# A planner's order of feed-forward work, products per head group, narrow reciprocals and a layer norm aggregated on GpSimd, in a two-layer graph network on one core

## The chip, the core and the metric

The kernel runs on one core of a Trainium2 chip. The metric is the device time of one execution in microseconds; three executions of the kernel before took 3080.15, 3081.23 and 3081.99 us, so the median is 3081.23 us. The core's engines are TensorE (PE in the profile; its weight loads are PEld), VectorE (DVE), ScalarE (ACT), GpSimd (POOL) and SyncE (SP), which here issues the DMAs. Each takes its instructions in the order of the program and waits for the others on semaphores.

## The reference

64 graphs of 256 nodes with 256 features go through two layers. All arithmetic is in float32.

```
# layer 0: two graph attentions, then a feed-forward
h = gat(x, adj, W1, a1);  h = gat(h, adj, W2, a2)
    # gat: Wh = h @ W; e = leaky_relu(Wh @ a[:F] + (Wh @ a[F:]).T); masked where adj <= 0;
    #      softmax over axis 1; then att @ Wh
h = layernorm(x + h) * g_ln1 + b_ln1
x = layernorm(h + relu(h @ w_ff1 + b_ff1) @ w_ff2 + b_ff2) * g_ln2 + b_ln2
# layer 1: attention of 8 heads with a value matrix for each relation r = 0..3
attn = softmax(q k^T / sqrt(32))
out = sum over r of (attn * (adj == r)) @ (x @ Wv[r] + bv[r])
x = layernorm(x + out @ Wo + bo) * g1 + beta1
x = layernorm(x + gelu(x @ W1 + b1) @ W2 + b2) * g2 + beta2
```

The feed-forward layers are 1024 wide. The adjacency has only the values 0 and 1, so of the four relations two remain.

## The kernel before

**Tiling and stages.** The graphs are taken in 32 pairs. A pair goes through four stages: `gat_layers`, `feed_forward` of layer 0 (ReLU), `attention`, and `feed_forward` of layer 1 (GELU). A pair is one Python generator, `whole_way`; each `yield` ends one step of TensorE work and names what the next step waits for: events, a stage to be alone in ("gat", "ff" and "attention": one pair at a time), and the number of PSUM banks needed of eight.

**What sets the order.** `run` is a planner that runs when the program is built. It keeps a clock for every engine, goes through four pairs at a time (`together`), and chooses the next instruction by estimated times. TensorE steps come from the generators; everything else is a piece handed over by `put(engine, us, emit, *events, rank=...)`, where `us` is the estimated cost. Of the pieces that are ready on an engine, the lowest rank goes first, and among equals the one ready earliest. Of TensorE's steps that have been ready for `SLACK` = 0.3 us, line by line:

```
g = going[min(sure, key=lambda n: (going[n][0] is besides, "ff" in (going[n][2] or ()) or alone.get("ff") is going[n][0], n))
          if sure else min(times)[1]]
```

So the pair that is in a feed-forward, in any part of it, comes after all other pairs. The order found is then fixed by `keep_order`: every engine executes it as it stands, whatever the actual times are.

**Feed-forward.** Its first product (FF1, line 689) is made in blocks with seven products in place of eight, class `Blocks`: p1 to p7, twice (`a` and `b`, two slabs each), in the order of line 710. p6 waits for the copy of p1's result (`copy`, line 695, on ACT), p7 for p6's copy, p4 for p7's copy; p5 and p3 wait for additions on DVE (line 393). Activations are at line 701. The second product (FF2, line 720) is for each graph b two halves j of eight matrix products, ordered in two parts of four; it waits for activations only in the first graph. Right after the products of a graph, its sum with the rows (`add_rows`, line 571) and its layer norm are handed to the planner. A float32 matrix product counts as two matmul instructions in the profile.

**Layer norm.** `layernorm` handles one graph, two tiles of 128 rows: on DVE `bn_stats` and `bn_aggr` for each tile (lines 581 and 582), on GpSimd four small operations on 128x2 values (lines 587 to 590; line 589 is the power -0.5), on ACT the normalisation (line 594). Then `transposed` turns the rows on DVE in 32x32 blocks (line 623, into the single buffer `yb`), stores them to DRAM and gathers them back by four DMAs on SP (line 628 and after); `scaled` (line 604) applies gain and bias on GpSimd. For a few pairs at the start and the end (`hurried`), the transposition is made on TensorE (line 655) instead.

**Attention.** q, k and v are made with `Blocks` too (lines 764 and 769). `scores(n)` handles a group of four heads of one graph, n = 0 to 3: 16 tiled matmuls of 32 rows (line 809) into four banks; ACT's Exp in two halves of two activations (line 818, tile `a`); on DVE the mask and the sums of halves (lines 822 and 826, tiles `m` and `h`). `products(n)` makes 80 tiled matmuls of 32 columns: line 840 for the values, line 843 for the sums with a matrix of ones, whose result stands in 32 equal rows for each head. Then DVE's reciprocal of 256 columns (line 852), the product (line 853), and on ACT a `check` of the sums' size (line 850), which reads both the sums and the reciprocals and frees the bank. The products are planned in twos: products(0) and products(1) in one step when all their masks are there, then scores(2) and scores(3), then products(2) and products(3).

At the end a flag is computed from the checks; for the present inputs it leaves the second, general program unused.

Of the kernel before, what the change touches and what calls it, by code (L numbers as in the profile page):

```python
# [27 lines left out]
HURRIED = 2  # L28
SLACK = 0.3
# [4 lines left out]
def two_layers(ctx: ExitStack, tc: tile.TileContext, t: dict, out: bass.AP, flag: bass.AP):  # L34
# [74 lines left out]

    w12 = const.tile([P, KC, D + 4], F32, name="w12")  # L110
# [31 lines left out]
    alone = {}  # L142
# [16 lines left out]
    def put(engine, us, emit, *events, rank=1, lag=0.2, kb=0, function=None, needs=None, frees=(), event=None):  # L159

        piece = {"engine": engine, "us": us, "emit": emit, "rank": rank, "lag": lag, "kb": kb, "function": function,
                 "needs": needs, "frees": frees, "event": event or Event(), "ready": 0.0, "missing": 0}
        for e in events:
            if e.time is None:
                piece["missing"] += 1
                e.then.append(piece)
            else:
                piece["ready"] = max(piece["ready"], e.time)  # L170
        if not piece["missing"]:
            waiting[engine].append(piece)
        return piece["event"]

# [39 lines left out]
    def run(besides, ways, together):  # L214
# [3 lines left out]
        going, ways = [[besides, *next(besides)]], iter(ways)  # L218
        together += 1
        while True:  # L220
# [23 lines left out]
            if engine == "tensor":  # L244
                sure = [n for at, n in times if at <= now - SLACK]
                g = going[min(sure, key=lambda n: (going[n][0] is besides, "ff" in (going[n][2] or ()) or alone.get("ff") is going[n][0], n))
# [11 lines left out]
            else:  # L258
                piece = waiting[engine].pop(min(able, key=lambda n: (waiting[engine][n]["rank"], waiting[engine][n]["ready"])))
# [77 lines left out]

    def block_sums(w, there):
# [34 lines left out]
    class Blocks:  # L373
# [5 lines left out]
        def __init__(self, second, first, begin, multiply, target, copy, corner, finished):  # L379
# [18 lines left out]
        def p1(self):  # L398
            yield *self.first, 1
            self.begin()  # L400
            self.u1 = self.copy(0, 0, self.product(1, "x", 0, True))

        def p2(self):
            yield [], None, 1
            there = self.product(2, "z", 1, True)
            self.c11 = self.add(0, 0, "z", self.u1, there)
            self.second.read_by_second(there)

        def p5(self):
            yield [self.c11, self.second.there[0]], None, 0  # L410
# [20 lines left out]
        def p3(self):  # L431
            yield [self.c22], None, 0
            self.add(0, 1, "z", self.u2, self.product(3, "z", 5), frees=["bank"])
# [56 lines left out]
    def gat_weights(y, at, at_home, ratio, there, to, b):  # L490
# [16 lines left out]
        def scale():  # L507
            for j in range(2):
                k = 2 * b + j
                nc.scalar.activation(y[:, k, :at], y[:, k, :at], AF.Copy, scale=of["rs"][:, j:j + 1])  # L510

        there = put("vector", 1.03, lambda: weigh(0), *there, rank=b / 2, needs="e")
        there = put("vector", 1.11, lambda: weigh(1), there, rank=b / 2, frees=["rows"] * b)
        return of, put("scalar", 0.8, scale, there, rank=0)
# [58 lines left out]
    def layernorm(r, b, *events):  # L573
        st = mv = rstd = less = None
        rows = [r[:, 2 * b + j, :] for j in range(2)]

        def statistics():
            nonlocal st, mv
            st, mv = small.tile([P, 2, 6], F32, name="st"), small.tile([P, 2, 2], F32, name="mv")
            for j in range(2):  # L580
                nc.vector.bn_stats(st[:, j, :], rows[j])  # L581
                nc.vector.bn_aggr(mv[:, j, :], st[:, j, :])  # L582

        def root():
            nonlocal rstd, less
            rstd, less = small.tile([P, 2], F32, name="rstd"), small.tile([P, 2], F32, name="less")
            nc.gpsimd.tensor_scalar(less, mv[:, :, 0], -1.0, None, ALU.mult)  # L587
            nc.gpsimd.tensor_scalar(rstd, mv[:, :, 1], EPS, None, ALU.add)
# [3 lines left out]
        def normalise():  # L592
            for j in range(2):
                nc.scalar.activation(rows[j], rows[j], AF.Identity, bias=less[:, j:j + 1], scale=rstd[:, j:j + 1])  # L594

        there = put("vector", 0.9, statistics, *events)
        there = put("gpsimd", 1.5, root, there, rank=0)
        return put("scalar", 0.8, normalise, there)
# [67 lines left out]
    def feed_forward(y, normal, w, func, relieved, pair, stage):  # L666

        w1, b1, w2 = w
# [3 lines left out]
        f, evacuated = [None] * NF, [[None] * NF for _ in range(2)]  # L672
# [5 lines left out]
        def slabs(t):  # L678

            rows, columns = [], (slice(0, N), slice(N, 2 * N))  # L680

            def begin():
                for c in range(2):
                    rows.append(work.tile([P, 2, 512], F32, name="ff", bufs=NF // 2))
                    for n in range(2):
                        f[t + n + c * half] = rows[c][:, n]
# [4 lines left out]
            def target(c, h):  # L691
                return rows[c][:, :, columns[h]]
# [4 lines left out]
            def activate(c, h, event, of=None):  # L697
                for n in range(2):
                    m, to = t + n + c * half, rows[c][:, n, columns[h]]
# [3 lines left out]
                        frees=["bank"] * (n and of is not None))  # L703

            first = ([normal[0], normal[1], relieved, second.there[0]], ["ff"]) if t == 0 else ([], None)
            blocks = Blocks(second, first, begin, multiply, target, copy, lambda of, event: activate(1, 0, event, of), activate)
# [5 lines left out]
        order, end = (0, 1, 4, 5, 2, 3, 6, 7), b.p3  # L712
        for b in range(2):
            for j in range(2):
                for part in (order[:half], order[half:]):
                    yield [evacuated[j][m] for m in part] if b == 0 else [], None, j == 0 and part[0] == 0
                    if j == 0 and part[0] == 0:
                        p2 = bank()
                    for m in part:
                        nc.tensor.matmul(p2[:, j * D:(j + 1) * D], lhsT=f[m][:, (2 * j + b) * P:(2 * j + b + 1) * P],  # L720
                                         rhs=w2[:, m, :], start=m == 0, stop=m == NF - 1)
                    there = took(0.43 * len(part))
                    if b == j == 0 and part[0] == 0:
                        yield from end()
                        frees_at(clock["tensor"], ["yT", "sums_yT"])
            normal[b] = layernorm(y, b, add_rows(y, p2, b, there, normal["scaled", b]))
            if onwards:
                transposed(y, normal[b], normal, b, pair, 1)
            else:
                normal[b] = scaled(y, ln[3], b, normal[b])  # L730
        done_with("ff")


    def attention(y, normal, pair, all_adj):
# [66 lines left out]
        def scores(n):  # L801
# [9 lines left out]
            there = took(1.08)  # L811
# [3 lines left out]
            def weight(q):  # L815
                a[n][q] = work.tile([P, 2, 512], F32, name="a", bufs=HQ)
                for k in range(2):
                    nc.scalar.activation(a[n][q][:, k], ps[2 * q + k], AF.Exp)  # L818
# [5 lines left out]
            def halves(q):  # L824
# [3 lines left out]
            there = [put("scalar", 0.96, lambda q=q: weight(q), there, rank=0, function="exp", needs="a", frees=["bank"] * 2)  # L828
                     for q in range(HQ // 2)]
# [3 lines left out]
        def products(n):  # L833
# [10 lines left out]
            there = took(2.2)  # L844
            frees_at(there.time, ["a", "m"] * (HQ // 2) + ["h"] * (HQ // 2 - 1))
            s, to = h[n][0][:, 0], qk[:, 0, c, b * N:(b + 1) * N]

            def check():
                for of, c in ((s, 0), (po[:, N:], 1)):
                    nc.scalar.activation(of, of, AF.Copy, accum_out=reach[:, pair, c, n:n + 1])  # L850

            there = put("vector", 1.68, lambda: nc.vector.reciprocal(s, po[:, N:]), there, rank=0)  # L852
            there = put("vector", 0.34, lambda: nc.vector.tensor_tensor(to, po[:, :N], s, ALU.mult), there, rank=0)
            put("scalar", 1.0, check, there, frees=["bank", "h"])
            return there
# [579 lines left out]
```

## Time and profile before

| Engine | busy, us | share of the span |
|---|---|---|
| TensorE matmuls | 3010.9 | 98% |
| TensorE weight loads | 2454.7 | 80% |
| VectorE | 2234.0 | 73% |
| ScalarE | 1835.1 | 60% |
| GpSimd | 1032.2 | 34% |

The profiled execution took 3077.64 us, and its span, from the first to the last instruction, is 3075.9 us. TensorE's granted clock was 0.994 of full speed over the span.

| Line, engine | what | count | busy, us | mean, ns |
|---|---|---|---|---|
| L720 PE | second feed-forward products, both layers | 4096 | 466.4 + 461.7 | 380 |
| L581 DVE | bn_stats | 512 | 208.4 | 407 |
| L582 DVE | bn_aggr | 512 | 93.2 | 182 |
| L587, L588 POOL | tensor-scalar on 128x2 | 256 each | 65.4, 60.1 | 255, 235 |
| L589 POOL | power on 128x2 | 256 | 189.1 | 739 |
| L590 POOL | product on 128x2 | 256 | 52.7 | 206 |
| L852 DVE | reciprocal of 256 columns | 128 | 224.1 | 1752 |
| L850 ACT | checks, two activations and two reads of sums | 128 | 53.0, 47.4, 24.6, 23.8 | 414, 370, 192, 186 |

A "busy" time of TensorE is the union of the matmuls' spans, which overlap; a mean is that of one matmul from its start to its modelled end. "A <- B: t, n, m" in a view of waits says that A's engine sat idle for t us in n places, m at the longest, until B released it. In the timeline a line gives the start, the duration, the engine, the line in the code and the number of merged instructions, and in brackets the idle time before it.

### The profile page before, as it was taken

To read this page: it belongs to the slowest core of one execution; us is meant where nothing else is said; L and a number is where in the kernel's file an instruction comes from. 1 tells how busy PE (TensorE), PEld (TensorE's weight loads), DVE (VectorE), ACT (ScalarE), POOL (GpSimd) and SP (SyncE) were. 2 spreads that over 40 slices of the span, in tenths; PEclk is the share of its full clock that TensorE was granted. 3 is DMA by queue.
4 is the path that set the end of the run, shared out by engine and by line. 5 is a ranking of instruction groups with operands and counts; after the bars stand their busy time and mean duration, and the time that the engine had idled before them with its cause. 6 is when DMAs were issued, how large, how long until landed. Compare 5 with 4: busy or idle time off the path is not lost.

```text
span 3075.9 us, 52423 instructions
## 1 busy us (share of the span) xinstructions
PE 3010.9 (98%) x19154; PEld 2454.7 (80%) x19154; DVE 2234.0 (73%) x4411; ACT 1835.1 (60%) x4186; POOL 1032.2 (34%) x1542
## 2 busy tenths in 40 slices
PE   7999999999999999999999999999999999999998
PEld 6877778877878788887888778878788778788876
DVE  5787766788776867768677676686776777767774
ACT  4556665656665566565756566565666565655654
POOL 1332244232423243232352322533325333233223
PEclk8999999999999999999999999999999999999999
DMA  6211132102321122211231122311213211121000
GB/s 181 73 51 36 56 124 79 46 28 75 109 66 50 61 76 80 73 49 56 76 99 60 42 70 69 97 66 50 66 54 96 82 53 57 62 93 58 32 1 22
DMA packets 211865, 205.76 MB, mean 67 GB/s; under 512 B 22928, under 2 KB 171280, under 8 KB 211600
## 3 DMA queue, kind: packets, MB, share of 16 engines
q1 hardware_dynamic: 211184, 202.06, 20.5%
q8 instruction: 154, 2.52, 0.3%
q14 instruction: 111, 0.91, 0.1%
q10 hardware_dynamic: 416, 0.26, 0.0%
HBM read 137.51 MB, written 64.73 MB: 66 GB/s over the span
## 4 chain that ended last, share of the span: by engine, by line
PE 79%; DVE 10%; ACT 3%; DMA 3%; POOL 2%; issue 2%; SPq 1%; DVEq 0%; POOLq 0%; ACTq 0%
PE ps L720 24%; PE ps L689 20%; PE ps L840 6%; PE ps L764 6%; PE ps L769 6%; PE ps L809 4%; PE ps L545 3%; PE ps L529 3%; PE ps L862 2%; PE ps L843 2%; DVE e L502 2%; DVE x L571 2%; DVE st L581 1%; PE ps L558 1%; DMA home<-yb 1%
## 5 line engine op out<-in xcount | busy, mean ns | idle before, releaser
L587 POOL TENSOR_SCALAR less<-mv 128x2 f32<-128x2 f32 x256 | 65.4, 255 | 1596.6 <-DVE mv L582 1561.4
L594 ACT ACTIVATE x<-x,less,rstd 128x256 f32<-128x256 f32 x512 | 279.3, 594 | 418.8 <-POOL less L590 414.9
L720 PE MATMUL ps<-w_L_gnn_w_ff,ff 128*128 128x256 f32 x2048 | 466.4, 380 | 0.0
L720 PE MATMUL ps<-w_L_gnn_W,ff 128*128 128x256 f32 x2048 | 461.7, 380 | 0.9 <-ACT ff L701 0.9
L720 PEld LDWEIGHTS ps<-w_L_gnn_W,ff 128*128 128x128 f32 x2048 | 386.9, 190 | 61.0 <-issue 5.4
L720 PEld LDWEIGHTS ps<-w_L_gnn_w_ff,ff 128*128 128x128 f32 x2048 | 387.9, 190 | 57.2 <-issue 4.3
L393 DVE TENSOR_TENSOR ff<-ps,ff 128x512 f32<-128x512 f32 x384 | 261.1, 683 | 163.6 <-PE ps L689 127.1
L822 DVE TENSOR_TENSOR m<-a,adj 128x1024 f32<-128x1024 f32 x256 | 325.4, 1271 | 20.6 <-ACT a L818 20.5
L689 PE MATMUL ps<-yT,w_L_gnn_W1p 128*128 128x256 f32 x1280 | 316.1, 384 | 10.9 <-ACT ff L695 7.4
L689 PE MATMUL ps<-yT,w_L_gnn_w_ff1p 128*128 128x256 f32 x1280 | 312.4, 384 | 12.3 <-ACT ff L695 12.3
L818 ACT ACTIVATE a<-ps 128x512 f32<-128x512 f32 x512 | 266.8, 603 | 68.0 <-PE ps L809 67.1
L689 PEld LDWEIGHTS ps<-yT,w_L_gnn_W1p 128*128 128x128 f32 x1280 | 238.3, 190 | 61.8 <-ACT ff L695 17.9
L689 PEld LDWEIGHTS ps<-yT,w_L_gnn_w_ff1p 128*128 128x128 f32 x1280 | 241.3, 191 | 56.6 <-ACT ff L695 16.7
L571 DVE TENSOR_TENSOR x<-ps,x 128x512 f32<-128x512 f32 x256 | 173.0, 680 | 152.4 <-PE ps L720 120.3
L695 ACT ACTIVATE ff<-ps 128x512 f32<-128x512 f32 x384 | 221.1, 589 | 92.0 <-PE ps L689 90.1
L604 POOL TENSOR_TENSOR x<-x,b_L_gnn_g_ln 128x512 f32<-128x512 f32 x128 | 168.7, 1318 | 274.5 <-DVE yb L623 138.3
L852 DVE RECIPROCAL h<-ps 128x256 f32<-128x256 f32 x128 | 224.1, 1752 | 49.1 <-PE ps L843 48.9
L581 DVE BATCH_NORM_STATS2 st<-x 128x6 f32<-128x256 f32 x512 | 208.4, 407 | 4.7 <-issue 0.4
L701 ACT ACTIVATE ff<-ff,c_L_gnn_b_ff 128x256 f32<-128x256 f32 x384 | 174.4, 509 | 49.4 <-DVE ff L393 48.8
L604 POOL TENSOR_TENSOR x<-x,b_L_gnn_g 128x512 f32<-128x512 f32 x128 | 166.1, 1298 | 94.4 <-ACT x L594 74.8
L589 POOL TENSOR_TENSOR rstd<-rstd,mhalf 128x2 f32<-128x2 f32 x256 | 189.1, 739 | 21.3
L701 ACT ACTIVATE ff<-ff,c_L_gnn_b 128x256 f32<-128x256 f32 x384 | 172.0, 502 | 31.6 <-DVE ff L393 31.0
(138 smaller groups left out, 5499.8 us busy)
## 6 DMA issues: line engine op xcount, KB each, us to landing
home<-yb SPq DMA_DIRECT2D x182, 256.0 KB, 2.0
yT<-home SPq DMA_DIRECT2D x728, 64.0 KB, 2.0
rows<-row SPq DMA_DIRECT2D x60, 512.0 KB, 3.8
input<-in_xT SPq DMA_DIRECT2D x32, 512.0 KB, 4.0
x<-in_x SPq DMA_DIRECT2D x32, 512.0 KB, 4.1
out<-x SPq DMA_DIRECT2D x32, 512.0 KB, 2.9
input<-in_adjT SPq DMA_DIRECT2D x30, 512.0 KB, 4.1
v<-in_adjT SPq DMA_DIRECT2D x2, 512.0 KB, 6.6
```

The lines of the kernel that those rows point to most:

```text
L393: nc.vector.tensor_tensor(self.target(c, h), self.bank[bank], self.target(c, h), ALU.add)
L571: return put("vector", 0.6, lambda: nc.vector.tensor_tensor(rows, p, rows, ALU.add), *events, frees=["bank"])
L581: nc.vector.bn_stats(st[:, j, :], rows[j])
L594: nc.scalar.activation(rows[j], rows[j], AF.Identity, bias=less[:, j:j + 1], scale=rstd[:, j:j + 1])
L604: nc.gpsimd.tensor_tensor(both, both, v.rearrange("p (k d) -> p k d", k=1).to_broadcast([P, 2, D]), op)
L689: nc.tensor.matmul(to, lhsT=w1[:, a, (t + slab) * P:(t + slab + 1) * P], rhs=b, **flags)
L695: return put("scalar", 0.5, lambda: nc.scalar.activation(target(c, h), blocks.bank["x"], AF.Copy), event, rank=-1)
L701: evacuated[h][m] = put("scalar", 0.4, lambda m=m, to=to, source=source: nc.scalar.activation(to, source, func, bias=b1[:, m:m + 1]), even ...
L720: nc.tensor.matmul(p2[:, j * D:(j + 1) * D], lhsT=f[m][:, (2 * j + b) * P:(2 * j + b + 1) * P], rhs=w2[:, m, :], start=m == 0, stop=m == N ...
L818: nc.scalar.activation(a[n][q][:, k], ps[2 * q + k], AF.Exp)
L822: nc.vector.tensor_tensor(m[n][q], a[n][q], adj, ALU.mult)
L852: there = put("vector", 1.68, lambda: nc.vector.reciprocal(s, po[:, N:]), there, rank=0)
```

## The change

- **Order of the feed-forward.** A pair that is in FF1 now comes before all other pairs, one that has reached FF2 (it stands in `filling`) after all others. FF1's tiles are laid out by block (c, h) and not by slab; FF2 is moved into `by_eight`, and both graphs' layer norms are handed over after both graphs' products.
- **Attention.** products(n) are steps of their own, each waiting only for its own masks; scores(2) follows products(0) and scores(3) products(1). scores(0) is planned after a_.p3 and b_.p4.
- **Reciprocals.** The sums are transposed in 32x32 blocks on DVE, one column of each block is copied (8 columns), inverted, and transposed back with a broadcast. The checks read the 8 columns, and the bank is freed by the product.
- **Layer norm.** bn_aggr is left out; nine small operations on GpSimd combine the two halves of bn_stats' result.
- **Pieces.** `put_each` hands over a piece in parts, each a piece of its own that keeps the first one's place: Exp, the scaling of the attention rows (`gat_weights`), statistics and normalisation. Some estimated costs differ.
- **Code that no stage uses.** `SEVEN` is empty, so `by_seven`, `last_weights` and `last_sums` aren't called, and no `Blocks` has a `seed`. The scratch of dynamic DMAs is set to 1024 bytes a partition.

```diff
-    def put(engine, us, emit, *events, rank=1, lag=0.2, kb=0, function=None, needs=None, frees=(), event=None):
+    def put(engine, us, emit, *events, rank=1, lag=0.2, kb=0, function=None, needs=None, frees=(), event=None, behind=None):
...
+        piece["first"] = behind.piece["first"] if behind else piece
+        piece["event"].piece = piece
...
+    def put_each(engine, us, emits, *events, rank=1, frees=(), needs=None, function=None):
+
+        before = None
+        for emit in emits[:-1]:
+            before = put(engine, us, emit, *events, rank=rank, lag=0.0, needs=needs, function=function, behind=before)
+            events, needs = [before], None
+        return put(engine, us, emits[-1], *events, rank=rank, frees=frees, function=function, behind=before)
+
...
+        def degree(g):
+            if g[0] in filling:
+                return 2
+            return 0 if "ff" in (g[2] or ()) or alone.get("ff") is g[0] else 1
...
-                g = going[min(sure, key=lambda n: (going[n][0] is besides, "ff" in (going[n][2] or ()) or alone.get("ff") is going[n][0], n))
+                g = going[min(sure, key=lambda n: (going[n][0] is besides, degree(going[n]), n))
...
-                piece = waiting[engine].pop(min(able, key=lambda n: (waiting[engine][n]["rank"], waiting[engine][n]["ready"])))
+                piece = waiting[engine].pop(min(able, key=lambda n: (waiting[engine][n]["rank"], waiting[engine][n]["first"]["ready"])))
...
-                nc.vector.bn_aggr(mv[:, j, :], st[:, j, :])
...
-            nc.gpsimd.tensor_scalar(less, mv[:, :, 0], -1.0, None, ALU.mult)
-            nc.gpsimd.tensor_scalar(rstd, mv[:, :, 1], EPS, None, ALU.add)
+            halves = [st[:, :, 3 * n + 1:3 * n + 3] for n in range(2)]
+            nc.gpsimd.tensor_tensor(apart, halves[0][:, :, 0], halves[1][:, :, 0], ALU.subtract)
+            nc.gpsimd.tensor_tensor(both, *halves, ALU.add)
+            nc.gpsimd.tensor_tensor(apart, apart, apart, ALU.mult)
+            nc.gpsimd.tensor_scalar(rstd, both[:, :, 1], 1.0 / D, EPS, ALU.mult, ALU.add)
+            nc.gpsimd.tensor_scalar(apart, apart, 0.25, None, ALU.mult)
+            nc.gpsimd.tensor_scalar(less, both[:, :, 0], -0.5, None, ALU.mult)
+            nc.gpsimd.tensor_tensor(rstd, rstd, apart, ALU.add)
             nc.gpsimd.tensor_tensor(rstd, rstd, mhalf[:, :2], ALU.pow)
             nc.gpsimd.tensor_tensor(less, less, rstd, ALU.mult)
...
-        there = put("vector", 0.9, statistics, *events)
-        there = put("gpsimd", 1.5, root, there, rank=0)
-        return put("scalar", 0.8, normalise, there)
+        there = put_each("vector", 0.35, [lambda j=j: statistics(j) for j in range(2)], *events)
+        there = put("gpsimd", 2.7, root, there, rank=0)
+        return put_each("scalar", 0.5, [lambda j=j: normalise(j) for j in range(2)], there)
...
+        yield from (by_seven if stage in SEVEN else by_eight)(y, normal, f, evacuated, w2, w2_there, b)
+        for g in range(2):
+            normal[g] = layernorm(y, g, *normal["added"][g])
+            if onwards:
+                transposed(y, normal[g], normal, g, pair, 1)
+            else:
+                normal[g] = scaled(y, ln[3], g, normal[g])
+        filling.clear()
+        done_with("ff")
+
+    def by_eight(y, normal, f, evacuated, w2, w2_there, last):
+
+        half, order, normal["added"] = NF // 2, (0, 1, 4, 5, 2, 3, 6, 7), []
+        filling.append(alone["ff"])
+        for g in range(2):
             for j in range(2):
                 for part in (order[:half], order[half:]):
...
+            normal["added"].append([add_rows(y, p2, g, there, normal["scaled", g])])
...
-            there = took(1.08)
+            there = took(1.13)
...
-            there = [put("scalar", 0.96, lambda q=q: weight(q), there, rank=0, function="exp", needs="a", frees=["bank"] * 2)
-                     for q in range(HQ // 2)]
+            there = [put_each("scalar", 0.48, [lambda q=q, k=k: weight(q, k) for k in range(2)], there, rank=0, function="exp",
+                              needs="a", frees=["bank"] * 2) for q in range(HQ // 2)]
...
-            there = took(2.2)
+            there = took(2.34)
...
+            def invert():
+                both.append(small.tile([P, 2, N // 32], F32, name="inverse", bufs=4))
+                nc.vector.transpose(s, po[:, N:])
+                nc.vector.tensor_copy(both[0][:, 1], blocks[:, :, 0])
+                nc.vector.reciprocal(both[0][:, 0], both[0][:, 1])
+                nc.vector.transpose(blocks, both[0][:, 0].rearrange("p (g i) -> p g i", i=1).to_broadcast([P, N // 32, 32]))
...
-            there = put("vector", 1.68, lambda: nc.vector.reciprocal(s, po[:, N:]), there, rank=0)
-            there = put("vector", 0.34, lambda: nc.vector.tensor_tensor(to, po[:, :N], s, ALU.mult), there, rank=0)
-            put("scalar", 1.0, check, there, frees=["bank", "h"])
-            return there
+            there = put("vector", 1.3, invert, there, rank=0)
+            put("scalar", 0.4, check, there, rank=3)
+            return put("vector", 0.34, lambda: nc.vector.tensor_tensor(to, po[:, :N], s, ALU.mult), there, rank=0, frees=["bank", "h"])
...
-        for step in (a_.p1, b_.p1, a_.p2, a_.p6, b_.p2, a_.p5, b_.p6, a_.p7, b_.p5, a_.p4, b_.p7, lambda: scores(0), a_.p3, b_.p4,  b_.p3, lambda: scores(1)):
+        for step in (a_.p1, b_.p1, a_.p2, a_.p6, b_.p2, a_.p5, b_.p6, a_.p7, b_.p5, a_.p4, b_.p7, a_.p3, b_.p4, lambda: scores(0), b_.p3, lambda: scores(1)):
...
-        for n in (0, 2):
-            yield [*masked[n], *masked[n + 1], ready["v", 0, n // 2], ready["v", 1, n // 2]], None, 2
-            divided += [products(n), products(n + 1)]
-            if n == 0:
-                for later in (2, 3):
-                    yield from scores(later)
+        for n in range(4):
+            yield [*masked[n], ready["v", 0, n // 2], ready["v", 1, n // 2]], None, 1
+            divided.append(products(n))
+            if n < 2:
+                yield from scores(n + 2)
```

## The prediction

> **What bounds the kernel now.** I read the page's first part, then PE's waits after the first 100 us, then the order of time around the places where PE stands or changes its kind of work, and last the chain of waits at the end.
>
> ```profile
> PE 3010.9 (98%) x19154; PEld 2454.7 (80%) x19154; DVE 2234.0 (73%) x4411; ACT 1835.1 (60%) x4186; POOL 1032.2 (34%) x1542
> ...
> PE ps L689 <- ACT ff L695: 23.5, 31, 1.7
> PE ps L545 <- ACT xw L510: 2.6, 1, 2.6
> ...
> PEld ps L689 <- ACT ff L695: 44.3, 55, 2.1
> ```
>
> TensorE is the bound; no other engine is near. So the change can gain only the time in which PE stands, and it loses whatever it adds to PE. From the trace's start times, a full-array matmul pass follows the last after 216 ns (four in 0.86 us). Counting all that stands over this between full-array passes gives 51 us after the first 100 us: 44 at L689 (the first feed-forward product), 7 elsewhere. The weight loads' 44.3 us are the same stall as PE's 23.5: a weight load held by a wait costs about 0.3 us on top of the wait. The first 100 us hold another 22 us of such stalls and the last PE instruction ends 12.6 us before the end of the span.
>
> One such stall, of 1.5 us, in order of time:
>
> ```profile
> 1316.57 1.08 ACT L594 ACTIVATE x<-x,less,rstd 128x256 f32<-128x256 f32 x2
> ...
> 1317.56 0.90 ACT L701 ACTIVATE ff<-ff,c_L_gnn_b_ff 128x256 f32<-128x256 f32 x2
> 1318.35 1.06 ACT L695 ACTIVATE ff<-ps 128x512 f32<-128x512 f32 x2
> 1318.50 1.28 POOL L604 TENSOR_TENSOR x<-x,b_L_gnn_g_ln 128x512 f32<-128x512 f32 x1
> 1318.99 0.73 PEld L689 LDWEIGHTS ps<-yT,w_L_gnn_w_ff1p 128*128 128x128 f32 x4 [1.75 <-ACT ff L695]
> 1318.99 1.13 PE L689 MATMUL ps<-yT,w_L_gnn_w_ff1p 128*128 128x256 f32 x4 [1.34 <-ACT ff L695]
> ```
>
> The copy that PE needs (L695) stands in ACT's queue behind two normalisations (L594), and the chain of waits leads from those through four layer norms in a row on GpSimd (L587 to L590, each 1.65 us from start to start). PE has nothing else planned there. In the steady part the same stalls come back every 374 us, that is with every four pairs of graphs (1317, 1691, 2066, 2441).
>
> Tiled products and full-array products in order of time on PE:
>
> ```profile
> 1011.07 1.07 PE L840 MATMUL ps<-a,v 128*32 128x256 f32 x16
> 1011.96 1.05 PE L840 MATMUL ps<-m,v 128*32 128x256 f32 x16
> 1012.82 0.61 PE L843 MATMUL ps<-h,ones 128*32 128x256 f32 x8
> 1013.25 1.05 PE L840 MATMUL ps<-a,v 128*32 128x256 f32 x16
> ...
> 1015.53 1.99 PE L862 MATMUL ps<-w_L_gnn_Wo,qk 128*128 128x256 f32 x8
> 1017.36 1.92 PE L529 MATMUL ps<-w,input 128*128 128x260 f32 x8
> ```
>
> The first group of heads takes 2.18 us to the start of the second, the second 2.28 to the start of L862, and L862's eight passes take 1.83 where 8 x 0.216 is 1.73. So leaving the tiled form costs 0.10 + 0.10, and entering it, by the trace's starts, 309 ns instead of 216, 0.09.
>
> The end, from the chain of waits:
>
> ```profile
> 3063.28 0.69 DVE x L571
> ...
> 3065.34 0.22 POOL less L587
> ...
> 3066.94 0.49 ACT x L594
> ...
> 3068.11 1.26 POOL x L604
> ```
>
> **What the Trainium skill says.** "TensorEngine Tiling (Array Packing)", Key Properties: a change of the tiling mode drains TensorE. The trace agrees: 0.09 us in, 0.20 out. "PSUM — Partial Sum Buffer", Engine vs sequencer instructions: the queues of ScalarE, VectorE and GpSimd are strict FIFO; the stall above, a copy behind a normalisation that waits for GpSimd, is that. "ScalarE: Activation LUTs", What ACT_TABLE_LOAD costs: 1283 ns for a load; the trace has 1283 too, 96 times. "VectorE: DVE Perf Modes", The TRN2 errata — SBUF-src ops pay a fixed extra latency per instruction: a fixed cost for each instruction, then a cost per element. The trace agrees: a transpose of 64 columns takes 240 ns and one of 512 takes 702.
>
> **The change part by part.** The sum is made against the profiled execution, 3077.64 us (span 3075.9, 1.7 around it); the median of the runs is 3081.23, 3.6 above. No matmul is removed or added. by_seven, last_weights, last_sums and the seed path are called only for stages in SEVEN, which is empty: nothing. The smaller scratch of the DMA setting: POOL issues no DMA in this trace, so I take nothing, between -1 and +1.
>
> *Order of the feed-forward.* Now every step of a feed-forward stands behind all other pairs' work, so it runs when nothing else is there, and the stalls of its dependent products (p6, p7, p4 wait for copies) lie bare. Afterwards p1 to p4 go first, with other pairs' steps left over to fill their waits, and the second products, 13.8 us without any wait (64 passes), come last and serve as a reserve. The 64 feed-forwards take 12 to 25 us for the first part today where its 56 passes need 12.1. At best all of the 51 us goes. Against that: at the end of a reserve the other pairs are all blocked, so the next first part may again find no filler. I take half, -26; bounds 0 and -45.
>
> *Products per head group.* L840/L843's 128 groups stand in 64 back-to-back pairs. If each pair is split by full-array work, one more exit and entry come in: 0.10 + 0.10 + 0.09, about 0.3 us, x 64 = +20. But scores(n + 2) may now follow products(n) directly if four banks are free, which saves the exit's second half and the entry, 0.2 us, up to twice a pair of graphs: 64 x 0.2 = 13 less (eight such neighbours exist already, so 11). Bounds +9 and +20, I take +13.
>
> *Layer norm on GpSimd.* bn_aggr goes from DVE (512 x 182 ns = 93 us). L587 to L590's four small operations (255 + 235 + 739 + 206 = 1.43 us) become nine: three of the tensor-scalar kind at about 0.24, five at 0.21, the power 0.74 = 2.5 us, and 0.07 us between neighbours. One layer norm thus holds GpSimd for 3.05 us instead of 1.65, its latency grows by 1.4 less 0.4 for the aggregations, +1.0. GpSimd's load is 1032 + 256 x 1.07 = 1306 us, 42%: no bound. In the middle other pairs' work on PE hides it; without that cover it is what blocks ACT's queue in the stall shown. At the start, pair 0's first norm lies bare: +1.
>
> *Norms after both halves.* Today the first half's norm is put out before the second half's products, afterwards after them. The transposes share one yb buffer and one SP queue (store, then four gathers a half), so a stage's hand-over lengthens by some 3 to 5 us; three other pairs hide that, and if not, the price is that of the slower rival. At the end nothing hides it. Today: last product, add, statistics, 1.6 on GpSimd, normalise, two scalings of 1.26. Afterwards the first norm's GpSimd part ends about 2.4 us after the last product, the second's runs 3.05 to about 5.4 after it, and four scalings of 1.34 follow (10.8) where today's last ends 7.5 after it: +3.
>
> *Reciprocals of 8 columns.* L852 (1752 ns) becomes two transposes of 256 columns (between the 240 and 702 ns rows: 0.44 each), a copy and a reciprocal of 8 columns (near L505's 166 ns): 1.25. DVE -0.5 x 128 = -64 us; DVE falls to about 2077. The checks (L850) shrink on ACT from 1.16 to 0.78 us: -49 us. Banks and h are free before the check. All beside PE: 0, and part of why half the stalls may go.
>
> *Pieces.* Exp, scalings, statistics and normalisations become two pieces each, so an urgent copy waits for one activation (0.6) and not for two. Against it, a Gelu may fall between two Exps: each such turn is two loads of 1.28 us on ACT, which has 40% to spare. 0, between -3 and +5.
>
> Sum: -26 + 13 + 1 + 3 = -9, about 3069 against 3077.64 and 3072 against the median.
>
> **The rivals.** *Slower: mode changes and the longer norm.* All 64 pairs of products are split (+20), the end costs +3, the start +1; and GpSimd's 3.05 us per norm, of which two now come in a row exactly when the next feed-forward's first products run, holds ACT's normalisations and the copies behind them. The planner books 2.7, so two in a row are 0.7 late. If each of the 64 feed-forwards pays that, less the 0.3 us of slack that it plans with, that is +26 and eats the order's -26: 3081 + 24 = 3105. Where half of them pay, 3092. It decides once the remaining stalls exceed 51 - 24 = 27 us. For it: GpSimd's chain already ends in the stall shown, and ACT waits 414.9 us for it. Against it: most norms have other work ahead.
>
> *A wash.* A third of the stalls goes (-17), which +13 + 4 eat: 3081. For it: the steady pattern loses only about 1.3 us for each pair of graphs, and PE is at 99% there.
>
> *Twice the gain.* Nearly all stalls go (-45) and scores follow products (+9 + 4): 3049. For it: the last feed-forward of all, which runs alone and without others' work on ACT, stalls for under 1 us.
>
> **How the numbers follow.** Faster at about half the stalls 0.43, nearly all 0.09, a wash 0.19, slower 0.29. The likeliest one's own range is 3062 to 3076. Ten per cent at each side are cut off: 3048 to 3100. About 0.2% (6 us) is what can be told from no change: faster 0.51, same 0.20, slower 0.29.
>
> **What would show it.** Right: PE's waits for L695's successor and the weight loads' 44.3 us halved; 64 or more separate clusters of tiled products; the last product to the end 15 to 16 us instead of 12.6; DVE near 2080 and GpSimd near 1300 us. Wrong: the weight loads' waits at the first products as large as now or larger, with ACT standing before its normalisations for GpSimd; new waits of PE at attention's products; or the products still in pairs.

## The result, and the profile after

The changed kernel takes 3064.08 us (median of four, 3063.49 to 3066.88) against 3081.61 us for the kernel before, run beside it: a ratio of 0.9952, 95% interval 0.994 to 0.9964. The prediction said 3072, between 3048 and 3100. The profiled execution went from 3077.64 to 3063.49 us, its span from 3075.9 to 3061.6, 14.3 us less; the prediction's sum was 9 less.

From the page of the changed kernel, the engines' busy time:

```profile
PE 3007.5 (98%) x19154; PEld 2451.5 (80%) x19154; DVE 2114.7 (69%) x4283; ACT 1771.4 (58%) x4182; POOL 1265.7 (41%) x2822
```

PE's waits after the first 100 us (total us, how many, the longest):

```profile
PE ps L731 <- ACT ff L737: 15.6, 12, 2.0
PE ps L731 <- DVE ff L424: 1.6, 4, 0.4
```

And those of the weight loads:

```profile
PEld ps L731 <- ACT ff L737: 25.6, 25, 2.4
```

L731 is what L689 was, L737 the copy that was L695. The weight loads' wait for the copies fell from 44.3 us in 55 places to 25.6 in 25. What held the copies changed too. From each such copy one can walk back along ACT's queue to the last instruction before which ACT stood idle. Before, 19.8 of the 44.3 us led to a normalisation (L594) that waited for GpSimd. Now 19.8 of the 25.6 lead to a scaling of attention rows (L551) that waited for VectorE, 3.7 to an activation that waited for VectorE, and 1.8 to a normalisation. Now the kinds of work on PE, from the timeline of the changed kernel:

```profile
533.27 1.07 PE L960 MATMUL ps<-a,v 128*32 128x256 f32 x16
534.15 1.05 PE L960 MATMUL ps<-m,v 128*32 128x256 f32 x16
535.02 0.61 PE L963 MATMUL ps<-h,ones 128*32 128x256 f32 x8
535.56 1.15 PE L929 MATMUL ps<-qk 32*128 32x256 f32 x16
536.64 1.07 PE L960 MATMUL ps<-a,v 128*32 128x256 f32 x16
...
540.01 3.72 PE L778 MATMUL ps<-w_L_gnn_w_ff,ff 128*128 128x256 f32 x16
543.57 2.75 PE L731 MATMUL ps<-yT,w_L_gnn_w_ff1p 128*128 128x256 f32 x12
```

A group's products are followed at once by the next scores: this holds for 64 of the 128 groups, which are all that can be, and in 22 of them products follow again. The tiled work stands in 179 separate clusters now, in 194 before. And the second products (L778) run straight into the next feed-forward's first ones (L731): all 64 feed-forwards follow one another without a gap, where before there were up to 26 us of other work between two.

Where the 14.3 us went, from the times between the starts of neighbouring PE passes after the first 100 us. "Stalls" is what exceeds the ordinary time between two passes, passes at half the clock among it; "changes of mode" is all time of tiled passes, their edges and the slow second pass behind them.

| us | before | after | difference |
|---|---|---|---|
| stalls | 51.3 | 29.6 | -21.7 |
| tiled passes and changes of mode | 509.0 | 514.6 | +5.6 |
| full-array passes after 100 us (what the start left over) | 2401.5 | 2402.9 | +1.4 |
| last PE pass to the end | 12.7 | 12.9 | +0.2 |

The end, from the timeline of the changed kernel:

```profile
3041.92 0.69 DVE L612 TENSOR_TENSOR x<-ps,x 128x512 f32<-128x512 f32 x1 [4.56 <-PE ps L778]
3042.64 0.75 DVE L622 BATCH_NORM_STATS2 st<-x 128x6 f32<-128x256 f32 x2
...
3049.62 0.75 DVE L622 BATCH_NORM_STATS2 st<-x 128x6 f32<-128x256 f32 x2
...
3050.45 0.20 POOL L629 TENSOR_TENSOR apart<-st 128x2 f32<-128x2 f32 x1 [0.70 <-DVE flag L1130]
3050.60 0.20 POOL L630 TENSOR_TENSOR both<-st 128x4 f32<-128x4 f32 x1
...
3052.72 0.19 POOL L637 TENSOR_TENSOR less<-less,rstd 128x2 f32<-128x2 f32 x1
3052.95 1.09 ACT L640 ACTIVATE x<-x,less,rstd 128x256 f32<-128x256 f32 x2 [5.88 <-POOL less L637]
```

The first graph's statistics start 0.03 us after its sum, 7 us before the second's, although the planner got them only after the second products. What counts on the chip is the place in VectorE's queue, and nothing stood between. The nine operations take 2.47 us from the start of the first (3050.45) to the end of the last (3052.72 + 0.19), not 3.05: L629 and L630, which don't depend on each other, start 0.15 us apart.

### The profile page after: what moved, and what is told of

It reads as the page before. It is cut to its first block, busy times and chain, and to the rows that moved or that the text cites. A ratio compares the mean times of both kernels' runs of the same rounds, so it can differ in the third digit from the quotient of the medians.

```text
span 3061.6 us, 53294 instructions
## 1 busy us (share of the span) xinstructions
PE 3007.5 (98%) x19154; PEld 2451.5 (80%) x19154; DVE 2114.7 (69%) x4283; ACT 1771.4 (58%) x4182; POOL 1265.7 (41%) x2822
## 3 DMA queue, kind: packets, MB, share of 16 engines
q1 hardware_dynamic: 211184, 202.06, 20.7%
## 5 line engine op out<-in xcount | busy, mean ns | idle before, releaser
L629 POOL TENSOR_TENSOR apart<-st 128x2 f32<-128x2 f32 x256 | 52.8, 206 | 1541.6 <-DVE st L622 1540.9
L778 PE MATMUL ps<-w_L_gnn_w_ff,ff 128*128 128x256 f32 x2048 | 470.1, 381 | 0.0
L778 PE MATMUL ps<-w_L_gnn_W,ff 128*128 128x256 f32 x2048 | 467.3, 381 | 0.0
L778 PEld LDWEIGHTS ps<-w_L_gnn_w_ff,ff 128*128 128x128 f32 x2048 | 385.6, 190 | 65.1 <-issue 14.3
L778 PEld LDWEIGHTS ps<-w_L_gnn_W,ff 128*128 128x128 f32 x2048 | 385.9, 190 | 63.7 <-issue 12.7
L640 ACT ACTIVATE x<-x,less,rstd 128x256 f32<-128x256 f32 x512 | 287.6, 592 | 97.4 <-POOL less L637 97.2
L942 DVE TENSOR_TENSOR m<-a,adj 128x1024 f32<-128x1024 f32 x256 | 315.9, 1234 | 14.9 <-ACT a L938 14.1
L731 PE MATMUL ps<-yT,w_L_gnn_w_ff1p 128*128 128x256 f32 x1280 | 311.9, 382 | 0.9 <-ACT ff L737 0.6
L731 PE MATMUL ps<-yT,w_L_gnn_W1p 128*128 128x256 f32 x1280 | 308.7, 381 | 0.0
L737 ACT ACTIVATE ff<-ps 128x512 f32<-128x512 f32 x384 | 223.3, 587 | 136.3 <-PE ps L731 135.5
L731 PEld LDWEIGHTS ps<-yT,w_L_gnn_w_ff1p 128*128 128x128 f32 x1280 | 243.1, 191 | 39.7 <-ACT ff L737 3.7
L731 PEld LDWEIGHTS ps<-yT,w_L_gnn_W1p 128*128 128x128 f32 x1280 | 242.3, 190 | 38.3 <-issue 3.3
L551 ACT ACTIVATE xw<-xw,rs 128x258 f32<-128x258 f32 (+1 forms) x256 | 116.9, 503 | 260.8 <-DVE rs L547 260.8
L622 DVE BATCH_NORM_STATS2 st<-x 128x6 f32<-128x256 f32 x512 | 193.9, 413 | 11.7
L743 ACT ACTIVATE ff<-ff,c_L_gnn_b 128x256 f32<-128x256 f32 x384 | 176.6, 502 | 39.8 <-DVE ff L424 37.2
L636 POOL TENSOR_TENSOR rstd<-rstd,mhalf 128x2 f32<-128x2 f32 x256 | 189.5, 740 | 20.1
L650 POOL TENSOR_TENSOR x<-x,b_L_gnn_g 128x512 f32<-128x512 f32 x128 | 163.6, 1281 | 80.3 <-DVE yb L669 37.6
L650 POOL TENSOR_TENSOR x<-x,b_L_gnn_g_ln 128x512 f32<-128x512 f32 x128 | 166.2, 1301 | 71.8 <-DVE yb L669 57.4
```

Source lines behind the costliest of these rows:

```text
L636: nc.gpsimd.tensor_tensor(rstd, rstd, mhalf[:, :2], ALU.pow)
L650: nc.gpsimd.tensor_tensor(both, both, v.rearrange("p (k d) -> p k d", k=1).to_broadcast([P, 2, D]), op)
L731: nc.tensor.matmul(to, lhsT=w1[:, a, (t + slab) * P:(t + slab + 1) * P], rhs=b, **flags)
L737: return put("scalar", 0.5, lambda: nc.scalar.activation(target(c, h), blocks.bank["x"], AF.Copy), event, rank=-1)
L743: evacuated[h][m] = put("scalar", 0.4, lambda m=m, to=to, source=source: nc.scalar.activation(to, source, func, bias=b1[:, m:m + 1]), even ...
L778: nc.tensor.matmul(p2[:, j * D:(j + 1) * D], lhsT=f[c][j][:, k, g * P:(g + 1) * P], rhs=w2[:, m, :], start=m == 0, stop=m == NF - 1)
```

## The experiments

The theory first: the order of the feed-forward saves the stalls. The rival: lighter VectorE and ACT save them. When the first four runs showed that the parts don't add up, a third joined: the planner. While the program is built, it keeps TensorE's clock and so books idle time itself. That is no measurement of the chip; it is the kernel's own account of an order. It books 26.1 us of idle TensorE after 100 us for the kernel before and 0.6 for the changed one. What a kernel's stalls on the chip exceed this by is called lateness here: work that came later than the planner had estimated. Lateness is a difference of two sums and not measured for itself. The last table of this section sets stalls and booked idle beside each other.

**The new order alone.** The kernel before, with

```diff
-                g = going[min(sure, key=lambda n: (going[n][0] is besides, "ff" in (going[n][2] or ()) or alone.get("ff") is going[n][0], n))
+                g = going[min(sure, key=lambda n: (going[n][0] is besides, degree(going[n]), n))
...
-        ... a_.p4, b_.p7, lambda: scores(0), a_.p3, b_.p4,  b_.p3, lambda: scores(1)):
+        ... a_.p4, b_.p7, a_.p3, b_.p4, lambda: scores(0), b_.p3, lambda: scores(1)):
```

> The kernel before with the new order of the feed-forward alone (first products first, second ones last; scores(0) planned after a_.p3 and b_.p4, as the change has it, because the new order needs the banks). Theory 'order': the stalls at the first products are saved by the order, so this kernel has most of the change's gain: about 3062 us, 3055 to 3068, PE stalls after 100 us down from 51 to 30 us or less. Rival 'lighter engines': the shorter reciprocals, the missing bn_aggr and the pieces made the copies come in time, and the order alone gives little: 3075 to 3083 us, stalls above 42 us.

3074.33 us, ratio 0.9983 (0.9976 to 0.9989). From PE's waits in this run:

```profile
PE ps L695 <- ACT ff L701: 16.1, 15, 3.0
PE ps L772 <- DVE qk L399: 3.7, 2, 1.9
...
PE ps L777 <- DVE v L399: 3.3, 3, 1.2
```

Stalls at the first products (here L695) fell from 44 to 27 us, but others came at attention (L772 and L777, 10 us), and all stalls are 50.0. The order brings a third of the gain by itself. That is far from the first theory; the time lies just under the rival's range, and the stalls above its 42 us.

**The old order in the changed kernel.** The first line of that diff turned round.

> The changed kernel with the old order of the feed-forward (all of it after other pairs' work). Theory 'order': the gain is lost, 3078 to 3088 us, and with the products of single groups it can be slower than before; stalls after 100 us near 50 us again. Rival 'lighter engines': the gain stays, 3062 to 3069 us, stalls near 30 us.

3216.51 us, ratio 1.0443 (1.0429 to 1.0457): 150 us more than the changed kernel, some 26 times what the order gains alone, and outside both ranges. PE's waits in this run:

```profile
PE ps L731 <- DVE qk L983: 38.0, 14, 3.4
PE ps L731 <- ACT ff L737: 36.1, 33, 2.6
PE ps L599 <- ACT xw L551: 10.0, 22, 1.0
```

The first is new: first products wait for VectorE's quotient at the end of a group's products (L983), which frees their bank. The mean granted clock fell from 0.993 to 0.981. After 100 us the trace has 18 stretches of 3.4 to 10.2 us at half clock, each with a stall of about 1 us or more in the 8 us before it; the changed kernel has two. Passes at half pace cost some 24 us of the time.

**Products in twos.** The changed kernel with the loop of before:

```diff
-        for n in range(4):
-            yield [*masked[n], ready["v", 0, n // 2], ready["v", 1, n // 2]], None, 1
+        for n in (0, 2):
+            yield [*masked[n], *masked[n + 1], ready["v", 0, n // 2], ready["v", 1, n // 2]], None, 2
```

> The changed kernel with the products of two head groups in one step again, scores(2) and scores(3) after them. Theory 'mode changes are the price of single groups': 64 exits between full-array and tiled work of 0.11 us go, clusters stay about as many, so 3057 to 3062 us. Rival 'single groups release a, m and h sooner and keep PE fed': 3066 to 3075 us, with new stalls or later feed-forwards.

3112.21 us, ratio 1.0108 (1.0092 to 1.0124), outside both ranges. Changes of mode do cost 9 us less (505.8 against 514.6), as the first theory has it; but stalls are 82 instead of 30. The price of single groups is real and small. That what they release early keeps PE fed, as the rival has it, is not shown: products in twos drew another order, in which the planner books 39.1 us itself.

**bn_aggr on VectorE again,** with its own estimates (0.45 us a tile, 1.5 us on GpSimd):

> The changed kernel with bn_aggr on VectorE again and four small operations on GpSimd instead of nine (planned at 0.45 us per tile and 1.5 us). Theory 'beside PE': the place of the aggregation is hidden, 3061 to 3067 us. Rival 'the longer norm holds the copies behind it on ACT' (the slower rival of the prediction): without it the remaining 28 us of stalls at the first products fall to 15 or less, 3048 to 3056 us. Rival 'VectorE's load matters': 3068 to 3075 us.

3070.58 us, ratio 0.9973 (0.9963 to 0.9983): 2 thousandths worse than the change. Another order came out, with 15.7 us of booked idle, 11.3 of it between 250 and 290 us; after 400 us it stalls less than the changed kernel. So this run mixes the place of the work and the order. The next one separates them.

**bn_aggr on VectorE in the same order.** As the last, but estimates stay at 0.35 and 2.7, so that the order is the changed kernel's, instruction by instruction, but for the norms' own:

```diff
             nc.vector.bn_stats(st[:, j, :], rows[j])
+            nc.vector.bn_aggr(mv[:, j, :], st[:, j, :])
...
+            nc.gpsimd.tensor_scalar(less, mv[:, :, 0], -1.0, None, ALU.mult)
+            nc.gpsimd.tensor_scalar(rstd, mv[:, :, 1], EPS, None, ALU.add)
             nc.gpsimd.tensor_tensor(rstd, rstd, mhalf[:, :2], ALU.pow)
```

> The changed kernel with bn_aggr on VectorE and four small operations on GpSimd, but with the estimated costs of the changed kernel left as they are, so that the planner finds exactly the changed kernel's order. It separates what the aggregation's place costs on the chip from what it does to the order. Theory 'the order decides, the engines have room': 3058 to 3067 us. Rival 'the nine operations hold ACT and the copies': 3056 us or less, with stalls at the first products halved from 28 to 14 us. Rival 'VectorE's load matters': 3070 us or more.

3078.63 us, ratio 1.0003 (0.9994 to 1.0011): all of the change's gain is gone, by 93 us on an engine that is busy for 71% of the time. Clusters and changes of mode are as in the changed kernel; stalls are 41.3 us instead of 29.6. The weight loads' waits of this run, and ACT's:

```profile
PEld ps L725 <- ACT ff L731: 45.1, 48, 1.7
```

```profile
ACT ff L737 <- DVE ff L424: 152.4, 140, 7.7
```

And the same wait of ACT in the changed kernel:

```profile
ACT ff L743 <- DVE ff L424: 113.7, 97, 6.4
```

ACT's activations wait longer for VectorE (152.4 us against 113.7 in the changed kernel), and behind them in its queue the copies (L731 in this kernel) that PE needs. Walked back as above, the 45.1 us of the weight loads all lead to an instruction of ACT that waited for VectorE. The rival 'VectorE's load matters' holds. The run takes the five extra operations off GpSimd at the same time, so it doesn't give the price of the longer norm by itself; in the changed kernel only the 1.8 us named above lead to a normalisation.

**More load on VectorE elsewhere.** The changed kernel with the first transpose of each reciprocal made twice, in the same order:

```diff
-                nc.vector.transpose(s, po[:, N:])
+                for _ in range(2):
+                    nc.vector.transpose(s, po[:, N:])
```

> The changed kernel with the first transpose of each narrow reciprocal made twice, costs and order left as they are: 128 x 0.44 = 57 us more on VectorE, about what the narrow reciprocals save against the wide ones. Theory 'VectorE's load decides how late the copies come' (93 us of it cost 15 us of stalls in the kernel with bn_aggr on VectorE in the same order): 57/93 x 15 = 9, so 3069 to 3077 us. Rival 'only the norm's own chain matters, attention's is hidden': 3062 to 3067 us.

3075.63 us, ratio 0.9991 (0.9984 to 0.9997). 57 us, far from any norm, cost 0.39% or 12 us; nine had been expected, within 3069 to 3077 us. So in this order VectorE's load costs about a sixth to a fifth of its time, wherever it lies.

**The old order and products in twos,** both as before the change, in the changed kernel:

> The changed kernel with the old order of the feed-forward and products in twos: in both it stands as the kernel before, only the operations, the pieces and scores(0)'s place are the changed ones. Theory 'planned idle': the planner itself books 78.6 us of idle TensorE after 100 us (0.6 in the changed kernel, 26.1 in the kernel before, 92.4 with the old order and single groups, which took 3216 us), so 3140 to 3200 us. Rival 'the old order is only bad together with single groups': 3075 to 3090 us, as the kernel before.

3138.24 us, ratio 1.019 (1.0174 to 1.0206), just under the theory's range. The order rules of the kernel before are bad with the changed operations and pieces.

**Norms handed over early.** The changed kernel with `layernorm` and what follows it called in `by_eight`, right after each graph's `add_rows`:

> The changed kernel with the first graph's layer norm handed to the planner right after that graph's second products, as before the change. The planner books 2.4 us of idle TensorE. Theory 'planned idle': 3062 to 3070 us, no difference that matters. Rival 'the late hand-over costs latency' (a step of the prediction): 3050 to 3059 us.

3074.58 us, ratio 0.9989 (0.9982 to 0.9996). Both theories missed: it is 0.37% slower than the change, with 2.4 us of booked idle and 39.8 of stalls, 8.6 of them in front of attention's first products. An earlier norm is no gain; why this order runs later against its estimates is not settled.

**Whole pieces.** `put_each` replaced by `put` of the whole in all four places:

> The changed kernel with the Exp, the scaling, the statistics and the normalisation as whole pieces again. The planner books 24.7 us of idle TensorE. Theory 'planned idle': 3078 to 3100 us. Rival 'pieces only matter on the chip, where a copy waits for one activation and not for two, at 0.6 us for each of some 30 stalls': 3064 to 3076 us.

3109.27 us, ratio 1.0097 (1.0082 to 1.0113), with 24.7 us booked and 69.5 us of stalls, above both ranges. Leaving out the pieces costs more than any number that was set for them, though again another order was drawn.

**VectorE's estimates 8% higher.** The changed kernel with one line:

```diff
+        us = us * (1.08 if engine == "vector" else 1.0)
         piece = {"engine": engine, "us": us, "emit": emit, "rank": rank, "lag": lag, "kb": kb, "function": function,
```

> The changed kernel with all estimated costs of VectorE 8% higher in the planner, nothing else; the planner then finds another order, with no idle TensorE after 100 us. Theory 'what is left of the stalls is VectorE running behind its estimates': stalls after 100 us fall from 26 to 15 us or less, 3046 to 3058 us. Rival 'the rest is ACT's queue and DMAs, or the chip's scatter': 3060 to 3070 us.

3043.88 us, ratio 0.9891 (0.9875 to 0.9906): 20 us better than the change, below the expected range. It beats both kernels. Its page, and PE's waits after 100 us:

```profile
PE 3001.3 (99%) x19154; PEld 2448.7 (81%) x19154; DVE 2089.7 (69%) x4283; ACT 1761.5 (58%) x4182; POOL 1234.8 (41%) x2822
```

```profile
PE ps L732 <- ACT ff L738: 3.0, 4, 1.5
PE ps L732 <- DVE ff L425: 0.7, 1, 0.7
```

Of 29.6 us of stalls 6.7 are left, with the same instructions. The estimates of the change are low for VectorE: 1.14 for the masks that take 1.23, 0.61 for the halves that take 0.71, 0.6 for the additions that take 0.69, 0.35 for statistics that take 0.41. With higher ones the planner can put an instruction that waits for VectorE later in ACT's queue, behind the copy and not before it; that this is how the 20 us came is inferred from the copies' waits, which all but vanish. Walked back as above, 4.0 us of the weight loads' waits still lead to a scaling (L552 here), 19.8 in the changed kernel. Only one factor was tried on the changed kernel, so a lucky order is not ruled out: the next two runs show how far two orders can lie apart.

**The same for the kernel before,** 6% and 8% higher:

> The kernel before, with all of VectorE's estimated costs 6% higher in the planner and nothing of the change. The planner books 23.3 us of idle TensorE after 100 us (26.1 before). Theory 'planned idle plus lateness': with honest estimates the lateness falls from some 25 us to about 10, so stalls of 33 instead of 51 us and 3060 to 3067 us: as much as the whole change brings. Rival 'the change's own parts are needed for it': 3075 to 3083 us.

3067.78 us, ratio 0.9964 (0.9952 to 0.9976), just above the theory's range: one factor in the kernel before brings three quarters of the change's gain. The stalls are 43.0 us, though, where the theory had 33; lateness fell to 20 us and not to 10.

> The kernel before, with VectorE's estimated costs 8% higher. The planner books 46.2 us of idle TensorE after 100 us. Theory 'planned idle plus lateness': 46 + 10 = 56 us of stalls, so 3080 to 3092 us, slower than before. Rival 'honest estimates pay whatever the planner books': 3050 to 3070 us.

3079.12 us, ratio 1.0001 (0.9993 to 1.0009), no change, and just under the theory's range. Two hundredths more in the factor, and 20.1 us more of booked idle than in the kernel before stand against 20.7 us less of lateness.

All kernels, in us: idle TensorE that the planner books after 100 us, and PE's stalls on the chip after 100 us, from the times between starts (waits at changes of mode included).

| kernel | booked | stalls | ratio |
|---|---|---|---|
| before | 26.1 | 51.3 | 1 |
| the change | 0.6 | 29.6 | 0.9952 |
| b_new_order | 31.3 | 50.0 | 0.9983 |
| a_old_order | 92.4 | 161.9 | 1.0443 |
| a_twos | 39.1 | 82.1 | 1.0108 |
| a_aggr_vector | 15.7 | 33.7 | 0.9973 |
| a_aggr_same_plan | 0.6 | 41.3 | 1.0003 |
| a_old_twos | 78.6 | 112.9 | 1.019 |
| a_norm_early | 2.4 | 39.8 | 0.9989 |
| a_whole_pieces | 24.7 | 69.5 | 1.0097 |
| a_invert_load | 0.6 | 41.5 | 0.9991 |
| v108 | 0.0 | 6.7 | 0.9891 |
| b106 | 23.3 | 43.0 | 0.9964 |
| b108 | 46.2 | 50.7 | 1.0001 |

Stalls grow with what is booked, with 5 to 70 us of lateness on top. It is least where VectorE's estimates were raised by 8% (7 and 5 us); the 20 us at 6% are no less than those of b_new_order and a_aggr_vector (19 and 18). Ratios are against the kernel before beside each run.

## Why the prediction was right, and where it was not

The bound was read rightly: only PE's stalls and what is added to PE could move the time, and they did. The prediction's parts come to -9 us, the measured ones to -14.5. That the total fits is in part luck: the half in the first part was a guess, and it covered parts that stand in the sum as nothing.

*Order of the feed-forward, -26.* The measured fall is 21.7 us, near the half that was taken. But the step gave it to the order alone, and that is wrong: alone the order brings 0.17% (5 us). The fall belongs to the whole, whose parts together leave the planner with 0.6 us to book.

*Products per head group, +13.* All changes of mode together cost 5.6 us more. The cost of an exit was right (the second pass behind a tiled cluster starts 320 ns after the first in both traces, 0.10 us late); the neighbours were mis-sized: 64 scores follow products, as many as can, where the +13 took few more than half. The lower bound (+9) counts all 64 and is still above the measured number. The clusters fell from 194 to 179; at the prediction's 0.3 us for an exit and an entry, an estimate, that is 4 us less.

*The end, +3.* Measured +0.2. The step that failed is "Norms after both halves: at the end nothing hides it". It took the planner's time for the chip's, and it added the nine operations up with a gap behind each.

*The start, +1.* The work done by 100 us lags by 1.4 us more than before, but not for the reason given. ACT's waits for the norms in this stretch fell from 4.6 to 3.0 us. What grew is a wait for the DMA of an adjacency (6.2 us instead of 3.3), and behind it PE's wait for the scaling at L586, 4.8 us instead of 1.4. The number was right by luck.

*Reciprocals and aggregation, "All beside PE: 0".* This failed. In an unchanged order 93 us of VectorE cost 0.5% (1.0003 against 0.9952) and 57 us cost 0.39%. The 69% of busy time hid that the order is fixed by estimates which VectorE doesn't keep; what it is late, ACT's queue passes on to PE. The prediction called it "part of why half the stalls may go" and so had it within the -26; there it is no small part. *Pieces, 0* is of the same kind: whole pieces cost 1.5%, in the order that the planner then finds. VectorE's busy time fell to 2114.7 us and not to 2080; one part of that is the narrow reciprocal, whose four steps take 1.37 us and not 1.25.

The slower rival (GpSimd's norm before ACT's copies) did not come: ACT's wait for the norms fell from 414.9 us to 97.2. Before:

```profile
ACT x L594 <- POOL less L590: 414.9, 152, 9.1
...
ACT xw L510 <- DVE rs L505: 100.3, 61, 9.0
```

In the changed kernel:

```profile
ACT xw L551 <- DVE rs L547: 260.8, 79, 12.0
...
ACT x L640 <- POOL less L637: 97.2, 60, 7.7
```

It fits that the norm takes 2.47 us where the planner books 2.7, but the hand-over counts as well: with the same nine operations and norms handed over early, ACT waited 199.5 us for them. In place of the normalisation stands the scaling of the attention rows (L551), which waits for VectorE. The stall that comes back in the changed kernel:

```profile
1539.25 0.91 ACT L551 ACTIVATE xw<-xw,rs 128x258 f32<-128x258 f32 x2 [9.14 <-DVE rs L547]
...
1540.36 0.91 ACT L551 ACTIVATE xw<-xw,rs 128x258 f32<-128x258 f32 x2 [0.20 <-DVE rs L547]
...
1541.18 1.06 ACT L737 ACTIVATE ff<-ps 128x512 f32<-128x512 f32 x2
1541.80 1.13 PE L731 MATMUL ps<-sums_yT,w_L_gnn_W1p 128*128 128x256 f32 x4 [1.88 <-ACT ff L737]
```

Same picture as before the change, with VectorE in GpSimd's place: a copy that was ready stands behind an instruction that isn't.

## What to carry to other kernels

Where a planner fixes each engine's order from estimates, look at two numbers: the idle time that it books itself, and how far each engine runs behind its estimates. Here an engine at 69% set part of the time by being late for instructions of another engine, behind which a copy stood that TensorE needed. Undoing one part under such a planner measures the new order and not the part; leave the estimates as they are, so that the order stays, to measure the part. Before rewriting operations, try the estimates of the busiest helper, at several values, since each draws a new order: 8% on VectorE gave more than the whole change on top of it, and nothing in the kernel before, where 6% gave 0.36%.

## What the runs showed of the hardware

An addition on VectorE with both inputs in SBUF can become much longer beside an operation on GpSimd. From the timeline of the changed kernel:

```profile
1528.77 1.47 POOL L650 TENSOR_TENSOR x<-x,b_L_gnn_g_ln 128x512 f32<-128x512 f32 x1
1529.13 1.38 DVE L390 TENSOR_TENSOR sums_yT<-yT,sums_yT 128x256 f32<-128x256 f32 x1
1530.19 1.45 POOL L650 TENSOR_TENSOR x<-x,b_L_gnn_beta 128x512 f32<-128x512 f32 x1
1530.43 1.49 DVE L390 TENSOR_TENSOR yT<-yT 128x256 f32<-128x256 f32 x1
```

And from the view of the tile yTa, the shortest, median and longest time in ns:

```profile
L390 DVE TENSOR_TENSOR yTa<-yTa x32: 408/420/1495, 131.9 to 2923.2; 128x256 f32<-128x256 f32 x32
```

In the timeline each addition ends 0.27 or 0.28 us after the operation on GpSimd beside it (1530.24 and 1530.51, 1531.64 and 1531.92). So it is over the whole trace: the 297 of the 384 additions at L390 that don't overlap with L650 take 446 ns at most, and all 73 that take more than 500 overlap with it and end some 0.3 us after it. The Trainium skill, "GPSIMD Engine Reference", 1. Specifications, says that the two engines share their SBUF interface and contend when VectorE has two SBUF inputs; the trace agrees, and adds the price: not a fixed factor, but the wait until GpSimd's operation is over. It is one reason why a fixed estimate for VectorE fails: the 384 additions take 201.1 us in the kernel before, 216.1 in the changed one and 179.8 in v108.
